# One group of leaky activations and its maximum moved behind ScalarE's two copies of the propagation's result

## The chip, the cores and the metric

The kernel runs on one core of a Trainium2 chip. Times are device microseconds (us) of a whole execution. TensorE, VectorE, ScalarE, GpSimd and SyncE are PE, DVE, ACT, POOL and SP in the profile; PEld is TensorE's weight load.

## The reference

Two graph layers work on 128 graphs of 128 nodes with 512 features, in float32. Layer 0 is graph attention with 8 heads, layer 1 a hypergraph convolution through a hidden width of 1024; each adds its input and normalizes.

```python
# layer 0: attention
dense = leaky_relu(e_self[..., :, None] + e_neigh[..., None, :], 0.2)
dense = dense + NEG_BIG * (1.0 - A)
att = softmax(dense, axis=-1)
out = relu(einsum('bhij,bhju->bhiu', att, feats) + b)
x = layernorm(x + out)
# layer 1: two hypergraph convolutions
h = layer_norm(relu(hypergraph_conv(x, adj, W1, b1)))
x = layernorm(x + hypergraph_conv(h, adj, W2, b2) + x)
```

## The kernel before

Graphs go in pairs, 64 of them, through a software pipeline that works on up to five pairs at once. The program is a list of steps with a lag (in pairs) and a time within a period; the list is sorted by (pair + lag) * 38.6 + time and issued. The times are no measurements: they only fix the order on each engine, and each engine keeps that order.

The steps of attention that matter: GpSimd adds the mask `neg` to the scores `nb`, ScalarE applies the leaky function, VectorE takes the maximum, ScalarE the exponential. Each is split into four groups (g = graph of the pair, q = half of the heads). The code here and below is shortened: lines that the argument does not need are left out, `...` stands for the rest of a line, and the comments are added.

```python
def masked(p, s, g, q):      # GpSimd, one instruction of 128x512
    nc.gpsimd.tensor_tensor(t, t, neg..., op=ALU.add)
def leaky(p, s, g, q):       # ScalarE, four instructions of 128x128
    for h in range(q * HH, (q + 1) * HH):
        nc.scalar.activation(t, t, AF.Prelu, bias=s["ft"][:, g, h, 0:1], alpha=SLOPE)   # (pair 0's special case cut)
def largest(p, s, g, q):     # VectorE, one reduction; exponential needs it
    nc.vector.tensor_reduce(s["nm"][:, g, hs], scores(p, s, g, hs)..., ALU.max, negate=True)

for (g, q), tm, (lag, tl), (lagx, tx), te, tt in (
    ((0, 0), 31.0, (1, 33.2), (1, 36.1), 2.7, 18.1), ((0, 1), 32.2, (1, 35.0), (1, 36.7), 4.6, 18.15),
    ((1, 0), 34.2, (1, 37.5), (2, 2.0), 7.8, 21.5), ((1, 1), 35.4, (2, 6.0), (2, 7.3), 7.9, 21.55),
):
    at(1, tm, masked, g, q); at(lag, tl, leaky, g, q); at(lagx, tx, largest, g, q)
    at(2, te, exponential, g, q)   # (rest of the loop cut)
```

The hidden product of an earlier pair stands at the same place of the period. TensorE makes the propagation `pz`, ScalarE copies it to `zT` (one copy for each graph), GpSimd forms four differences `zS`, and TensorE makes seven products in the order 1, 2, 6, 5, 7, 4, 3. Products 1 and 2 read graph 0 of zT alone; the third one issued, number 6, reads zS's second difference and adds to the bank `phX`, of which ScalarE must have copied product 1 first.

```python
at(3, 0.0, propagate, 0);  at(3, 0.9, propagate, 1)   # TensorE: pz
at(3, 1.1, z_evict, 0);    at(3, 2.0, z_evict, 1)     # ScalarE: zT <- pz
for i, t in enumerate((2.7, 3.4, 4.1, 4.8)):
    at(3, t, z_sums, i)                               # GpSimd: zS
chain("ph", 3, (2.0, 3.8, 5.6, 7.35, 9.1, 12.65, 14.4,   # TensorE: the seven products
                4.0, 7.5, 11.0), hidden, HALF)           # ScalarE: three copies of phX
rhs = {1: b[0][0], 2: b[0][1], 3: b[1][1], 4: t[:, 3], 5: t[:, 0], 6: t[:, 1], 7: t[:, 2]}[i]

@step(0, 38.4)
def mask(p, s):              # GpSimd; masked() reads it a period later
    nc.gpsimd.tensor_scalar(s["neg"], s["a"], -1.0, BIG, op0=ALU.add, op1=ALU.mult)
```

## Time and profile before

| | before |
|---|---|
| time, median of 3 runs | 2595.87 us |
| busy share PE / PEld / DVE / ACT / POOL | 97 / 88 / 74 / 59 / 71 % |
| steady period of a pair | 39.78 us |
| TensorE's idle time before the first hidden product | 56.3 us in 61 waits |

A group's line in the profile has the source line, engine, operation, tiles and count, then busy time and mean ns of one, then the idle time of the engine in front of the group and what ended it. Only idle time of the engine that bounds the kernel costs anything. The prediction below shows these lines; here is one view that it only mentions, the chain of work that ended last (shares of the span, by engine and by source line), of the kernel before:

```profile
PE 68%; ACT 13%; DMA 7%; issue 6%; DVE 2%; POOL 2%; SPq 1%; DVEq 0%; POOLq 0%; ACTq 0%
```

TensorE carries most of it, ScalarE the next largest part.

### The profile page before, as it was taken

The numbers are of one execution on the slowest core, as the hardware profiler recorded it, in microseconds if no ns is written. First come the engines' busy times: TensorE is split into PE (matmuls) and PEld (weight loads), VectorE is DVE, ScalarE is ACT, GpSimd is POOL, SyncE is SP. The second block draws the span as 40 slices with busy tenths as digits, with TensorE's granted clock in tenths as the row PEclk, the third lists the DMA queues.
The fourth block names the chain that finished last, engine by engine and source line by source line (L and its number), as shares of the span: only waits on it lengthen the run. The fifth ranks groups of instructions, "written<-read, shape, count | busy, mean of one in ns | idle before, by whom it ended". The sixth has DMA issues, their size and how long they took to land.

```text
span 2594.2 us, 48549 instructions
## 1 busy us (share of the span) xinstructions
PE 2513.1 (97%) x16349; PEld 2272.8 (88%) x16349; DVE 1915.8 (74%) x4332; ACT 1537.0 (59%) x4481; POOL 1833.0 (71%) x2058
## 2 busy tenths in 40 slices
PE   7999999999999999999999999999999999999998
PEld 5888888888888888888888888888888888888897
DVE  7877777777777777777777777777777777777765
ACT  4565665655655656656556566565565565665653
POOL 5777767776777677767766776777677767776774
PEclk9999999999999999999999999999999999999999
DMA  6544444445444454444444444444444444444431
GB/s 186 131 131 132 136 135 140 132 123 144 127 131 140 131 139 133 126 146 129 126 144 131 132 134 137 140 130 124 144 127 132 138 133 140 133 125 141 132 111 54
DMA packets 420840, 343.76 MB, mean 133 GB/s; under 512 B 141272, under 2 KB 370160, under 8 KB 420592
## 3 DMA queue, kind: packets, MB, share of 16 engines
q1 hardware_dynamic: 417120, 336.19, 43.8%
q10 hardware_dynamic: 3472, 4.47, 0.5%
q8 instruction: 131, 2.15, 0.3%
q14 instruction: 117, 0.96, 0.1%
HBM read 238.83 MB, written 101.71 MB: 131 GB/s over the span
## 4 chain that ended last, share of the span: by engine, by line
PE 68%; ACT 13%; DMA 7%; issue 6%; DVE 2%; POOL 2%; SPq 1%; DVEq 0%; POOLq 0%; ACTq 0%
PE phX L792 18%; PE phW L792 9%; PE pfX L473 8%; ACT nb L592 8%; PE pav L662 7%; PE pyX L473 6%; DMA x<-in_x_dram 6%; PE phY L792 4%; PE pq L919 4%; PE pfW L473 4%; PE pyY L473 3%; PE pfY L473 2%; ACT y L734 2%; POOL rsa L709 1%; ACT zT L769 1%
## 5 line engine op out<-in xcount | busy, mean ns | idle before, releaser
L792 PEld LDWEIGHTS phX<-zS,w_sb 128*128 128x128 f32 x3072 | 363.1, 192 | 33.0 <-issue 31.5
L329 ACT COPY py<-pyX 128x257 f32<-128x257 f32 x189 | 70.8, 375 | 539.2 <-PE pyX L473 513.6
L792 PE MATMUL phX<-zS,w_sb 128*128 128x128 f32 x3072 | 374.4, 275 | 2.2 <-POOL xS L455 1.3
L845 POOL TENSOR_TENSOR sq<-sq 128x512 f32<-128x512 f32 (+2 forms) x384 | 343.8, 895 | 37.6 <-ACT sq L833 17.5
L576 POOL TENSOR_TENSOR nb<-nb,neg 128x512 f32<-128x512 f32 x256 | 318.3, 1276 | 12.5 <-DMA nb<-rd 12.5
L592 ACT ACTIVATE nb<-nb,ft 128x128 f32<-128x128 f32 x1020 | 317.2, 388 | 7.1 <-POOL nb L576 7.1
L606 ACT ACTIVATE nb<-nb,nm 128x128 f32<-128x128 f32 x1024 | 320.5, 394 | 0.4 <-DVE nm L598 0.4
L709 POOL TENSOR_TENSOR rso<-veo,mhalf 128x2 f32<-128x2 f32 x63 | 44.2, 701 | 354.9 <-DVE veo L707 354.9
L598 DVE TENSOR_REDUCE nm<-nb 128x4 f32<-128x512 f32 x256 | 174.6, 683 | 116.0 <-ACT nb L592 56.4
L662 PEld LDWEIGHTS pav<-ft,eT 128*128 128x128 f32 x2048 | 248.3, 192 | 8.4 <-DVE eT L639 0.8
L662 PE MATMUL pav<-ft,eT 128*128 128x65 f32 x2048 | 242.5, 272 | 0.0
L473 PE MATMUL pyX<-w_sb,hS 128*128 128x257 f32 x1008 | 242.5, 382 | 0.0
L473 PE MATMUL pyX<-w_sb,h 128*128 128x257 f32 x1008 | 239.5, 380 | 0.5 <-ACT py L329 0.5
L822 ACT ACTIVATE h<-h,vecs 128x128 f32<-128x128 f32 x768 | 238.5, 392 | 2.2 <-DVE h L807 2.2
L473 PE MATMUL pyW<-w_sb,hS 128*128 128x256 f32 x1008 | 238.6, 378 | 0.2 <-DVE y L876 0.2
L473 PEld LDWEIGHTS pyW<-w_sb,hS 128*128 128x128 f32 x1008 | 190.7, 189 | 27.9 <-DVE y L876 0.7
L686 POOL TENSOR_TENSOR y<-y,b_bc 128x512 f32<-128x512 f32 x128 | 162.8, 1272 | 70.9 <-DVE y L677 70.9
L473 PEld LDWEIGHTS pyX<-w_sb,h 128*128 128x128 f32 x1008 | 186.4, 190 | 25.5 <-ACT py L329 0.9
L473 PEld LDWEIGHTS pyX<-w_sb,hS 128*128 128x128 f32 x1008 | 186.1, 190 | 24.3
L792 PE MATMUL phX<-zT,w_sb 128*128 128x128 f32 x1024 | 132.7, 283 | 56.3 <-ACT zT L769 56.3
L329 ACT COPY ph<-phX 128x512 f32<-128x512 f32 x192 | 112.5, 586 | 118.1 <-PE phX L792 118.1
L792 PEld LDWEIGHTS phX<-zT,w_sb 128*128 128x128 f32 x1024 | 120.7, 194 | 68.1 <-ACT zT L769 68.0
(167 smaller groups left out, 5778.4 us busy)
## 6 DMA issues: line engine op xcount, KB each, us to landing
nb<-rd SPq DMA_DIRECT2D x127, 512.0 KB, 6.7
ed<-nb SPq DMA_DIRECT2D x126, 512.0 KB, 2.6
eb<-ed SPq DMA_DIRECT2D x504, 128.0 KB, 2.9
x<-in_x_dram SPq DMA_DIRECT2D x64, 512.0 KB, 9.5
out_dram<-o SPq DMA_DIRECT2D x63, 512.0 KB, 2.8
xb<-in_x_dram SPq DMA_DIRECT2D x248, 128.0 KB, 3.1
a<-in_adj_dram SPq DMA_DIRECT2D x64, 128.0 KB, 8.2
w<-in_adj_dram SPq DMA_DIRECT2D x128, 64.0 KB, 7.3
```

The costliest lines, as they stand in the source:

```text
L329: nc.scalar.copy(t[:, :n], s[kind, "X"][:, :n])
L473: nc.tensor.matmul(to[:, :n], lhs[:, k, :], rhs[:, k, :n], start=bool(start) and k == 0, stop=(k == nk - 1), skip_group_check=True,)
L576: nc.gpsimd.tensor_tensor(t, t, neg[:, :, None, :].to_broadcast([P, NB, HH, B]), op=ALU.add)
L592: nc.scalar.activation(t, t, AF.Prelu, bias=s["ft"][:, g, h, 0:1], alpha=SLOPE)
L598: nc.vector.tensor_reduce(s["nm"][:, g, hs], scores(p, s, g, hs).rearrange("p b h j -> p h b j"), AX.XY, ALU.max, negate=True,)
L606: nc.scalar.activation(t, t, AF.Exp, bias=s["nm"][:, g, h:h + 1])
L662: nc.tensor.matmul(t[:, h * (U + 1):(h + 1) * (U + 1)], s["eT"][:, g, q * HH + h, :], s["ft"][:, g, q * HH + h, 2:], start=True, stop=True,)
L686: nc.gpsimd.tensor_tensor(s["y"][:, g, :], s["y"][:, g, :], b0_bc, op=ALU.add)
L792: nc.tensor.matmul(to[:, m * N:(m + 1) * N], w[:, k, m * P:(m + 1) * P], rhs[:, k, :], start=bool(start) and m == 0 and k == 0, stop=(k == ...
L822: nc.scalar.activation(dst[:, k, :], src[:, k, :], AF.Relu, bias=b1_sb[:, c:c + 1])
L845: nc.gpsimd.tensor_tensor(t[:, :n, :], t[:, :n, :], t[:, n:2 * n, :], op=ALU.add)
L919: nc.tensor.matmul(s["pq", g], s["R"][:, g, :], s["y2"][:, g, :, :QU], start=True, stop=True)
```

## The change

The intent is to let ScalarE copy zT before the leaky group of graph 1, heads 0 to 3, so that TensorE's first hidden product starts sooner. The group's maximum follows it in the program.

```diff
-        ((1, 0), 34.2, (1, 37.5), (2, 2.0), 7.8, 21.5), ((1, 1), 35.4, (2, 6.0), (2, 7.3), 7.9, 21.55),
+        ((1, 0), 34.2, (2, 2.05), (2, 2.1), 7.8, 21.5), ((1, 1), 35.4, (2, 6.0), (2, 7.3), 7.9, 21.55),
```

## The prediction

> **What bounds the kernel now.** I read the page's busy shares first, then the groups of TensorE by their idle time, then the chain of waits, then the timeline of one steady period of each engine.
>
> ```profile
> PE 2513.1 (97%) x16349; PEld 2272.8 (88%) x16349; DVE 1915.8 (74%) x4332; ACT 1537.0 (59%) x4481; POOL 1833.0 (71%) x2058
> ```
>
> TensorE (PE) is busy 97% of 2594.2 us, so about 81 us of the span is idle there. The kernel is 64 graph pairs in a software pipeline; from about 138 us to 2485 us each pair takes 39.78 us (the first matmul of phX starts at 1252.13 and 1291.91). The TensorE groups with idle time in front show where the idle part lies (idle is the second number after the bar):
>
> ```profile
> L792 PE MATMUL phX<-zT,w_sb 128*128 128x128 f32 x1024 | 132.7, 283 | 56.3 <-ACT zT L769 56.3
> L757 PE MATMUL pz<-R,y 128*128 128x128 f32 x1024 | 126.2, 277 | 6.0 <-ACT y L734 6.0
> ...
> L473 PE MATMUL pfX<-w_sb,xT 128*128 128x264 f32 x496 | 134.2, 393 | 0.0
> ```
>
> 56.3 us stand before the first hidden product of each pair, ended by ScalarE's copy of the propagation's result (zT, L769). Nearly every other group shows 0 to 2 us; the next largest, 8.1 us, is the first load. The chain of waits gives the same as a count: the wait occurs 61 times, and the weight loads see it as 68.0 us.
>
> ```profile
> PEld phX L792 <- ACT zT L769: 68.0, 61, 3.0
> ...
> PE phX L792 <- ACT zT L769: 56.3, 61, 2.8
> ```
>
> One of the 61 is 2.84 us (at 97.01 us, start-up); the other 60 are 0.88 to 0.90 us each. One period in the middle, from the timeline (start, length):
>
> ```profile
> 1289.08 1.95 PE L757 MATMUL pz<-R,y 128*128 128x128 f32 x16
> 1289.86 0.35 ACT L874 COPY y<-pyX 128x256 f32<-128x256 f32 x1
> 1290.11 1.28 ACT L592 ACTIVATE nb<-nb,ft 128x128 f32<-128x128 f32 x4
> 1291.29 1.05 ACT L769 COPY zT<-pz 128x512 f32<-128x512 f32 x2
> 1291.91 2.05 PE L792 MATMUL phX<-zT,w_sb 128*128 128x128 f32 x16 [0.88 <-ACT zT L769]
> 1292.23 1.28 ACT L606 ACTIVATE nb<-nb,nm 128x128 f32<-128x128 f32 x4
> 1292.90 1.15 POOL L780 TENSOR_TENSOR zS<-zT 128x256 f32<-128x256 f32 x1
> 1294.13 0.73 POOL L780 TENSOR_TENSOR zS<-zT,zS 128x256 f32<-128x256 f32 x1
> ...
> 1295.58 1.95 PE L792 MATMUL phX<-zS,w_sb 128*128 128x128 f32 x16
> ```
>
> The reader should see that four leaky activations (L592) stand between the copy of y and the two copies of zT, while TensorE's result for the first copy is ready early: the 16 matmuls of pz start 0.112 us apart, so graph 0's eight end at about 1289.08 + 7 x 0.112 + 0.275 = 1290.14. Those four activations are exactly the group that the change moves (graph 1, heads 0 to 3).
>
> **What the Trainium skill says.** "Perfetto Trace Analysis", section "Identifying the Most-Contended Engine", says that matmul busy time is a poor measure and that weight-load busy share is better; here that is 88%, so the choice of engine stands, with less certainty than 97% suggests. Its "Optimization Strategy" says to find the gaps on that engine and make what ends them start sooner, which is the change's intent. The same page, "DVE / Act Engine Instruction", puts semaphore propagation outside an instruction's recorded window; the trace agrees: phX starts a median of 0.052 us after the first zT copy ends, and I use 0.05 us for every hand-over. "SBUF — State Buffer", "Who interferes with whom", says that a VectorE instruction with two SBUF inputs and a GpSimd instruction that reads SBUF exclude one another. The trace agrees: the first zS subtraction takes 1.15 us here, where y's scaling runs on VectorE until 1293.46, and the second, undisturbed, 0.73.
>
> **The change part by part.** Nothing is added or removed: 62 x 4 activations and 62 reductions (pairs 2 to 63; the first two pairs have times or scaling of their own) get a new place. Their engine time is unchanged.
>
> On ScalarE the order becomes copy of y, two copies of zT, leaky group, exponentials. The y copy ends at 1290.21; graph 0's pz is ready at about 1290.14 + 0.05. So the first zT copy starts near 1290.2 instead of 1291.29 and, at 0.57 us, ends near 1290.77. TensorE would start phX back to back at the last pz matmul plus one step. In the 60 steady periods phX starts 1.167 us after the last pz matmul starts; one step is 0.112. **Ceiling: 1.167 - 0.112 = 1.055 us**, and the restart also costs something: the 32 matmuls from phX's first to the first on zS take 3.675 us where 32 steps are 3.576, so 0.10 us more is spared if no stall is left. The ceiling is 1.15 us a period, 69 us in all.
>
> It will not be reached, because of what comes next on TensorE. The third product needs zS's second difference, by GpSimd. That one ends at 1294.86, and not because zT was late: GpSimd works without a pause from 1284.99 (its power for rsa, four maskings, the small ops for rsh, the mask, then zS), with no wait for zT before zS: the second zT copy has ended at 1292.34, zS starts at 1292.90 as soon as the mask ends. What starts this block is VectorE's vea, which follows pyY's evaluation at 1281.76, itself released by TensorE. From pyY to pz TensorE has no pause, so GpSimd's zS keeps its distance to pz when zT comes early. Measured against phX's old start, zS's second difference ends at +2.968 us (median of the steady periods) and the third product starts at +3.675: today 0.707 us of slack.
>
> With phX at -1.055, the third product would be due at -1.055 + 3.576 = +2.521. zS lets it start at 2.968 + 0.05 = +3.02. **A new wait of about 0.50 us** replaces the 0.89 us one, with its own restart of 0.10 us. Net: 3.675 - (3.02 + 0.10) = **0.555 us a period**, x 60 = 33.3 us.
>
> Start-up period at 97.01 us: the gap of 2.84 us loses the four activations' 1.17 us (ScalarE's y copy ends there at 95.32, zT starts at 96.40); add 1.2 us. In the last changed period (2524.01) TensorE already starts phX without a gap: 0. Sum: 34.5 us. Predicted: 2595.9 - 34.5 = **2561 us**, a ratio of 0.987.
>
> What moves beside it: the second zT copy must wait for pz's end (1291.03), so ScalarE idles about 0.35 us and the leaky group ends near 1292.8. Its maximum on VectorE starts today at 1293.39, after y's scaling, so it still does not wait. The first phX copy comes at about 1293.95, ends at 1294.5, still ahead of the third product's overwrite at 1294.93. The next leaky group ends near 1296.85, and the second phX copy starts near 1297.05, which is TensorE's time; ScalarE's slack before it (0.64 us today) is used up, yet not overdrawn. VectorE before the second h sum loses its 0.21 us wait and comes about 0.36 us late relative to TensorE, but ScalarE works on the first relu group meanwhile, and VectorE waits 0.97 us for TensorE at the next h sum.
>
> **The rivals.** First, the full gain: zS does not bind, and 60 x 1.15 us make 2527 us (2.7% faster). For it: the change removes the only repeated TensorE gap. Against: the zS times above; it needs GpSimd to be early, and nothing in its 10 us block before zS is moved. It would also be right if the lengths shown for GpSimd are rough by half a microsecond.
>
> Second, the leaky group and its maximum become late work: ScalarE's extra idle and the chain leaky, exponential, phX copy delay the third product's bank or the store and re-read of the exponentials. ScalarE's slack in the stretch is 0.48 + 0.64 us today, of which about 0.35 is lost to waiting for pz and 0.5 because TensorE comes earlier. A shortfall of 0.3 us a period would leave about 2579 us. Against it: exponentials of graph 0 are ready earlier than before, by roughly the period's gain.
>
> Third, the pipeline is held by a transfer: nb's load must land before the masking. For: a large part of the chain that ended last is put down to an x load. Against: GpSimd waits for nb only once, at start-up (12.5 us), and in each period it waits 2.39 us for VectorE's vea. With a transfer bound the time would stay at 2596.
>
> **Range and chances.** The most likely size error is the hand-over and where zS ends, 0.1 to 0.2 us a period, 6 to 12 us in all. The second rival gives the upper side, half of the first the lower. So 2548 to 2577 us. Faster by over 2% needs less than 2544 us, 0.86 us a period: the zS bound would have to be mostly absent, 0.10. Slower by over 2% would need a new wait of over 1.7 us a period: 0.02. The rest is 0.88.
>
> **What would show it right or wrong.** The wait of phX on zT should fall from 56.3 us to nearly nothing (under 5), and a new wait of phX on POOL zS, about 60 times and 0.4 to 0.5 us each (25 to 30 us), should stand in its place. In the timeline zT's copies should start about 0.6 us before pz's last matmul with leaky after them, GpSimd should have no gap between its mask and zS, and the period should be near 39.22 us. I am wrong if no wait on zS appears (then the gain is nearer 60 us), if the first phX copy on ScalarE ends later than zS, or if VectorE's maximum waits for leaky and pushes the h sum behind phX.

## The result and the profile after

| | before | after |
|---|---|---|
| median, same rounds (4 runs each) | 2596.82 us | 2560.72 us |
| lowest to highest | 2595.8 to 2597.81 | 2559.9 to 2561.77 |
| ratio (95% interval) | | 0.9861 (0.9844 to 0.9878) |
| steady period, median | 39.778 us | 39.213 us |

Ratios are the mean time of one kernel's runs over that of the other's of the same rounds, so they are not quite the ratio of the medians quoted. The kernel is 1.4% faster, and clear of the noise.

Busy time on the page of the changed kernel:

```profile
PE 2516.7 (98%) x16349; PEld 2275.8 (89%) x16349; DVE 1914.3 (75%) x4332; ACT 1539.8 (60%) x4481; POOL 1832.7 (72%) x2058
```

The instructions are the same and each engine's busy time stays within 4 us; the shares rise because the span fell by 34.3 us. TensorE's groups (idle time is the second number after the bar):

```profile
L792 PE MATMUL phX<-zS,w_sb 128*128 128x128 f32 x3072 | 380.7, 277 | 19.0 <-POOL zS L780 17.2 <-POOL xS L455 1.3 <-ACT ph L329 0.5
...
L792 PE MATMUL phX<-zT,w_sb 128*128 128x128 f32 x1024 | 127.9, 278 | 1.7 <-ACT zT L769 1.7
```

The wait for zT fell from 56.3 to 1.7 us, and a wait for GpSimd's zS, which was not there before, stands in front of the products that read zS. The view of the waits counts it (us in total, times, longest):

```profile
PEld phX L792 <- POOL zS L780: 28.8, 61, 0.5
...
ACT zT L769 <- PE pz L757: 24.1, 66, 1.6
...
PE phX L792 <- POOL zS L780: 17.2, 61, 0.3
```

One steady period on the timeline of the changed kernel (start, length, engine):

```profile
1272.14 1.95 PE L757 MATMUL pz<-R,y 128*128 128x128 f32 x16
1272.93 0.35 ACT L874 COPY y<-pyX 128x256 f32<-128x256 f32 x1
...
1273.23 0.59 ACT L769 COPY zT<-pz 128x512 f32<-128x512 f32 x1
...
1273.92 2.00 PE L792 MATMUL phX<-zT,w_sb 128*128 128x128 f32 x16
...
1274.12 0.59 ACT L769 COPY zT<-pz 128x512 f32<-128x512 f32 x1 [0.31 <-PE pz L757]
...
1274.61 1.28 ACT L592 ACTIVATE nb<-nb,ft 128x128 f32<-128x128 f32 x4
...
1275.04 0.97 POOL L363 TENSOR_SCALAR neg<-a 128x256 f32<-128x256 f32 x1
...
1275.98 1.16 POOL L780 TENSOR_TENSOR zS<-zT 128x256 f32<-128x256 f32 x1
...
1277.22 0.72 POOL L780 TENSOR_TENSOR zS<-zT,zS 128x256 f32<-128x256 f32 x1
...
1277.99 2.05 PE L792 MATMUL phX<-zS,w_sb 128*128 128x128 f32 x16 [0.29 <-POOL zS L780]
```

phX follows pz at once. The mask and the two differences on GpSimd keep their place relative to pz: the second difference ends at 1277.22 + 0.72 = 1277.94, 0.05 us before the third product starts. Over the steady periods it ends 4.123 us after the last pz matmul starts, against 4.135 before; the third product starts a median of 0.053 us after it, against 0.706 before. The chain that ended last now has GpSimd where it had ScalarE:

```profile
PE 66%; POOL 23%; issue 8%; DVE 2%; DMA 1%; ACT 0%; SPq 0%; POOLq 0%; DVEq 0%; ACTq 0%
```

Where the 34.3 us between the two profiled spans came from, by the starts of phX on the timeline: the third pair's phX comes 1.6 us earlier (138.36 to 136.75), the 59 periods up to the 62nd pair's are 33.2 us shorter (2346.85 to 2313.64), and what follows it is 0.6 us longer (108.96 to 109.53), of which 0.4 us is the new wait in one more period (38.80 to 39.22 us).

### The profile page after: what moved, and what is told of

The parts are those of the page before. It is cut to its first block, busy times and chain, and to the rows that moved or that the text cites.

```text
span 2559.9 us, 48549 instructions
## 1 busy us (share of the span) xinstructions
PE 2516.7 (98%) x16349; PEld 2275.8 (89%) x16349; DVE 1914.3 (75%) x4332; ACT 1539.8 (60%) x4481; POOL 1832.7 (72%) x2058
## 4 chain that ended last, share of the span: by engine, by line
PE 66%; POOL 23%; issue 8%; DVE 2%; DMA 1%; ACT 0%; SPq 0%; POOLq 0%; DVEq 0%; ACTq 0%
PE phX L792 14%; POOL nb L576 11%; PE pyX L473 9%; PE phW L792 9%; PE pfX L473 9%; PE pav L662 8%; POOL zS L780 4%; PE pq L919 4%; PE pyY L473 4%; PE pfW L473 4%; POOL neg L363 2%; PE pfY L473 2%; POOL rsh L905 2%; POOL rsa L709 2%; DVE y L876 1%
## 5 line engine op out<-in xcount | busy, mean ns | idle before, releaser
L792 PE MATMUL phX<-zS,w_sb 128*128 128x128 f32 x3072 | 380.7, 277 | 19.0 <-POOL zS L780 17.2
L598 DVE TENSOR_REDUCE nm<-nb 128x4 f32<-128x512 f32 x256 | 174.6, 683 | 179.5 <-ACT nb L592 117.4
L627 DVE STREAM_TRANSPOSE eT<-eb 128x512 f32<-128x512 f32 x252 | 163.1, 684 | 0.8 <-DMA eb<-ed 0.7
L833 ACT ACTIVATE sq<-h 128x512 f32<-128x512 f32 x256 | 160.7, 629 | 2.1
L455 POOL TENSOR_TENSOR hS<-h 128x512 f32<-128x512 f32 x126 | 158.6, 1277 | 2.3 <-ACT h L822 2.3
```

The costliest lines, as they stand in the source:

```text
L627: nc.vector.transpose(s["eT"][:, g, hs, :].rearrange("p h (b i) -> p h b i", b=NB), s["eb", g][:, :, hs, :].rearrange("p b h j -> p h b j"),)
L792: nc.tensor.matmul(to[:, m * N:(m + 1) * N], w[:, k, m * P:(m + 1) * P], rhs[:, k, :], start=bool(start) and m == 0 and k == 0, stop=(k == ...
L833: nc.scalar.activation(s["sq"][:, g, q * KH // 2:(q + 1) * KH // 2, :], hid(s, g, q), AF.Square, scale=DH ** -0.5,)
```

## The experiments

The main theory: TensorE's wait for zT was on the path, the change removed it whole, and about half of the gain was given back because zS on GpSimd, which the change does not move, became the wait. The rivals: that ScalarE's order (its idle time before the second copy, the later copy of phX) is the limit and zS came last by chance; that more work on GpSimd costs time anywhere. Eight kernels were run, each in three rounds besides its profiled run; all gave correct results.

| run | median us | ratio to before (95%) | steady period us |
|---|---|---|---|
| mask_later | 2539.82 | 0.9779 (0.9765 to 0.9794) | 38.867 |
| between | 2561.6 | 0.9863 (0.9848 to 0.9878) | 39.226 |
| before_mask_later | 2596.44 | 0.9999 (0.9984 to 1.0014) | 39.777 |
| both | 2533.35 | 0.9754 (0.9737 to 0.977) | 38.759 |
| mask_twice | 2584.12 | 0.995 (0.9935 to 0.9964) | 39.580 |
| before_mask_twice | 2597.02 | 0.9999 (0.9984 to 1.0014) | 39.777 |
| behind_phx | 2560.83 | 0.9862 (0.9845 to 0.9878) | 39.214 |
| behind_phx_mask_later | 2527.9 | 0.9734 (0.9719 to 0.9749) | 38.667 |

The kernel before had medians of 2596.6 us in the rounds of the first four and 2597.37 us in those of the last four.

### mask_later: GpSimd's mask out of zS's way

On the changed kernel. The mask goes behind the four xS sums of its pair (6.1 to 8.2 in the program's times). The first two pairs, which have no xS sums, keep their place.

```diff
-    @step(0, 38.4)
     def mask(p, s):
...
+    at(0, 38.4, mask, until=2)
+    at(1, 8.3, mask, since=2)
```

> The changed kernel, with GpSimd's mask (0.97 us in front of zS) moved behind the four xS sums of its pair, where GpSimd has over 5 us free. Main theory, that zS's second difference is what the third product waits for: zS comes 0.5 us or more earlier, the wait of phX on zS falls from 17.2 us (matmuls) and 28.8 us (weight loads) to under 3 us each, and the period falls from 39.22 us to 38.7 to 38.85; the first copy of phX, which ends within 0.07 us of the third product, may show as a small wait. Time 2530 to 2540 us. Rival, that the order on ScalarE (its 0.31 us idle before the second zT copy, the later phX copy) is the limit and zS only came last by chance: the wait gets ScalarE's name, and the time stays at 2555 to 2562.

Measured 2539.82 us, at the upper edge of what was expected; the period of 38.867 us is just above it. The wait on zS is gone from the view of waits. Its timeline shows what remains:

```profile
1264.70 1.95 PE L794 MATMUL phY<-zT,w_sb 128*128 128x128 f32 x16
...
1265.90 0.57 ACT L329 COPY ph<-phX 128x512 f32<-128x512 f32 x1
...
1266.62 2.02 PE L794 MATMUL phX<-zS,w_sb 128*128 128x128 f32 x16
```

Sixteen matmuls take 16 x 0.112 = 1.79 us to issue, so the third product was due at 1266.49 and came at 1266.62. zS's second difference had ended a median of 0.88 us earlier; ScalarE's copy of phX ended at 1266.47. So zS was the limit, and the copy on ScalarE is the next one, 0.125 us later than the issue rate allows plus 0.07 us in the product's second matmul (0.184 us after the first instead of 0.112). The copy's hand-over is 0.144 us in the median, against 0.053 for zT and zS; which part makes it longer is open. That it is the copy is argued here; behind_phx_mask_later tests it.

### between: half of the reordering

On the changed kernel; the leaky group goes between the two copies of zT.

```diff
-        ((1, 0), 34.2, (2, 2.05), (2, 2.1), 7.8, 21.5), ...
+        ((1, 0), 34.2, (2, 1.5), (2, 2.1), 7.8, 21.5), ...
```

> The changed kernel, with the leaky group between the two zT copies instead of behind both: only one half of the change's reordering. Main theory: TensorE needs only the first copy for phX, and zS is held by GpSimd's own work and not by the second copy (which would end about 0.5 us before zS starts), so the time equals the changed kernel's, 2559 to 2563 us, and ScalarE's wait for pz before the second copy (24.1 us in all) is gone. Rival, that both copies had to come forward, or that ScalarE's idle costs time: slower by over 8 us in the first case, faster by over 5 us in the second.

Measured 2561.6 us, the changed kernel's time. ScalarE's wait for pz fell to 5.4 us, and TensorE's wait on zS stayed:

```profile
PE phX L792 <- POOL zS L780: 17.9, 61, 0.3
```

The first copy alone made the change's gain, and ScalarE's idle time before the second copy costs nothing as long as zS is late.

### before_mask_later: the second cure without the first

The same edit of the mask, on the kernel before.

> The kernel before, with only GpSimd's mask moved as in mask_later. Main theory: zS had 0.707 us of slack there and phX's start waited for zT, so earlier zS is worth nothing: 2594 to 2599 us. Rival, that GpSimd's load before zS costs time by itself (contention with VectorE's scaling of y, say) whatever the order on ScalarE: 10 us or more faster.

Measured 2596.44 us, no change. TensorE still waits 56.3 us for zT, and zS's slack before the third product grew to 1.180 us in the median. The mask's move is worth 21 us only after the leaky group has gone (2560.72 to 2539.82, medians of different rounds).

### both: group between the copies, mask later

> mask_later and between together on the changed kernel. Main theory: with zS early and the first phX copy about 0.35 us earlier too, TensorE runs from pz through all products without a gap: the period is 38.66 us (39.22 less 0.444 of wait and 0.10 of restart), 2525 to 2531 us, and faster than mask_later by up to 9 us. Rival (ScalarE's order is the limit): no better than between.

Measured 2533.35 us, 6.5 us better than mask_later but 2.4 us above the expected range; the period is 38.759 us, not 38.66. Its timeline:

```profile
1261.14 0.56 ACT L771 COPY zT<-pz 128x512 f32<-128x512 f32 x1
...
1261.78 0.81 POOL L782 TENSOR_TENSOR zS<-zT 128x256 f32<-128x256 f32 x1 [0.57 <-ACT zT L771]
...
1262.67 1.06 POOL L782 TENSOR_TENSOR zS<-zT,zS 128x256 f32<-128x256 f32 x1
...
1263.79 2.04 PE L794 MATMUL phX<-zS,w_sb 128*128 128x128 f32 x16
```

With the mask out of the way GpSimd is free before the second copy of zT, which the leaky group now delays: it waits 0.57 us for it. zS's second difference ends at 1263.73, only 0.06 us before the third product. No gap shows between the products, yet the product's second matmul comes 0.20 us after its first, instead of 0.112. That is the missing 0.09 us. The run taught that the order between, harmless while zS is held by the mask, is not harmless any more.

### mask_twice and before_mask_twice: more work in front of zS

The mask is computed twice with the same values, once on each kernel.

```diff
         nc.gpsimd.tensor_scalar(s["neg"], s["a"], -1.0, BIG, op0=ALU.add, op1=ALU.mult)
+        nc.gpsimd.tensor_scalar(s["neg"], s["a"], -1.0, BIG, op0=ALU.add, op1=ALU.mult)
```

> The changed kernel with GpSimd's mask done twice (the same values again), so that GpSimd carries more in front of zS. Main theory (zS sets the third product): each 0.1 us that zS comes later costs 0.1 us a period. The second mask takes 0.4 us alone; part of it may take the place of the time that zS's first difference now stands blocked (1.16 us against 0.73). So 0.25 to 0.8 us a period, 15 to 50 us slower than the changed kernel: 2576 to 2611 us; and the wait of phX on zS grows by the same amount as zS's delay in the trace. Rival (zS came last by chance): 2561 us, within 5 us.

Measured 2584.12 us, 23.4 us above the changed kernel (medians of different rounds). GpSimd's timeline in mask_twice:

```profile
1284.52 0.97 POOL L363 TENSOR_SCALAR neg<-a 128x256 f32<-128x256 f32 x1
1285.57 0.72 POOL L364 TENSOR_SCALAR neg<-a 128x256 f32<-128x256 f32 x1
1286.26 0.72 POOL L781 TENSOR_TENSOR zS<-zT 128x256 f32<-128x256 f32 x1
1287.06 0.73 POOL L781 TENSOR_TENSOR zS<-zT,zS 128x256 f32<-128x256 f32 x1
```

The second mask took 0.72 us, where 0.4 was expected, and spared the first difference its blocked time (0.72 instead of 1.16). Relative to pz, zS's second difference ends 4.491 us after pz's last matmul starts instead of 4.123: 0.368 us later. The period grew by 39.580 - 39.213 = 0.367 us. The delay arrives one for one, and the wait of phX on zS grew by as much, 0.37 us each (17.2 to 39.5 us in 61 waits):

```profile
PE phX L793 <- POOL zS L781: 39.5, 61, 0.7
```

> The kernel before with the mask done twice. Main theory: zS's second difference has 0.707 us of slack there, less 0.05 us of hand-over; a delay of 0.3 to 0.6 us is hidden: 2595 to 2600 us; only a delay over 0.65 us would show, by its excess. Rival, that more GpSimd work costs time anywhere: slower by the same 15 to 50 us as mask_twice is against the changed kernel.

Measured 2597.02 us against 2597.37 for the kernel before in the same rounds: nothing. zS ends at the same 4.491 us there, a delay of 0.356 us, and its slack falls from 0.706 to 0.350 us. The same work on the same engine costs 23 us in one kernel and shows no cost in the other.

### behind_phx and behind_phx_mask_later: the group behind the copy of phX as well

```diff
-        ((1, 0), 34.2, (2, 2.05), (2, 2.1), 7.8, 21.5), ...
+        ((1, 0), 34.2, (2, 4.05), (2, 5.95), 7.8, 21.5), ...
```

> The changed kernel with the leaky group moved on behind ScalarE's first copy of phX, and its maximum behind the first h sum; mask where it was. The first phX copy then comes over 0.5 us before it is needed. Main theory: zS still holds the third product, so no gain: 2558 to 2564 us, wait of phX on zS about 17 us. Rival (the leaky group on ScalarE is still in the way): faster by 10 us or more.

Measured 2560.83 us: no gain, wait of phX on zS 17.3 us. ScalarE's order is not the limit while zS is.

> behind_phx together with the mask moved behind the xS sums. mask_later lost 0.2 us a period to the first phX copy (third product 0.126 us late, 0.08 of restart), and the run with the group between the zT copies lost 0.10 because zS started later. Here neither should be left: period 38.66 to 38.69 us, 2525 to 2530 us, the fastest of all. If the maximum, now late, holds the exponentials or the h sum instead, 2535 us or more with a new wait named on ScalarE or VectorE.

Measured 2527.9 us (2527.67 to 2528.14), the fastest of all, 2.7% below the kernel before of the same rounds and, by the medians of different rounds, 1.3% below the changed one. The wait for zS has gone from its groups of TensorE (the 2.0 us left are three waits, which the kernel before has as well, at 2.2 us):

```profile
L794 PE MATMUL phX<-zS,w_sb 128*128 128x128 f32 x3072 | 374.4, 275 | 2.0 <-POOL neg L362 1.3 <-ACT ph L329 0.7
```

zS ends 0.748 us before the third product, the copy of phX about 1.0 us before it, and the steps from pz to phX, from product to product and within the third product are all 0.112 us. Together with mask_later this shows that the copy of phX was what mask_later still waited for: the mask stands alike in both, zS ends at the same place (2.98 us after pz's last matmul starts), and only the leaky group, and with it the copy, moved. The periods differ by 0.200 us, which is the 0.125 and 0.07 us seen in mask_later.

## Why the prediction was right

**The time.** 2561 us was predicted and 2560.72 measured; the range of 2548 to 2577 held.

**The gap that closes.** The step from pz to phX fell from 1.167 to 0.112 us as foreseen, and the first zT copy started at 1273.23, 0.69 us before phX and 0.58 before pz's last matmul (0.6 was written).

**The new wait.** zS's place relative to pz was assumed to stay; it moved by 0.012 us. mask_twice shows that a delay of zS reaches the period one for one, and mask_later, together with before_mask_later, shows that zS and not the load of GpSimd as such was the limit.

**The sum.** Predicted gain 0.555 us a period, measured 0.565. Its parts differ a little from those written. The new wait in front of the third product is a step of 0.556 instead of 0.112 us, so 0.444, not 0.50: the missing 0.05 is lost already in phX's second matmul (0.159 us after the first, instead of 0.112), though phX itself starts without a gap. So only 0.054 of the old restart's 0.10 us was spared: 1.055 + 0.054 - 0.444 - 0.101 = 0.564. The restart cost of 0.10 us was inferred from the length of 32 matmuls; it shows in the second matmul after a wait (0.213 us in both kernels). Start-up gave 1.6 us instead of 1.2, the end took 0.6 that was counted as 0. The mechanism held term by term, but that the total came within 1 us is in part luck: these errors cancel.

**Where the text was inexact.** It said that the new wait would show as 0.4 to 0.5 us each and 25 to 30 us in all. Weight loads show 28.8 us; the matmul row shows 17.2, 0.28 each. The matmul row counts idle time from the end that it records for the matmul before, 0.275 us after its start, while my 0.50 counts from the step; 0.556 - 0.275 = 0.281. The text should have said which row.

**What the hand-over is.** The prediction timed it to the first matmul and added a restart. The weight load in front of that matmul is what waits; it starts 0.05 us after the zT copy or the zS difference ends, and the second matmul follows that end by 0.266 us in the median wherever the product waited, and in no steady period of the ten kernels by less than 0.265. So in these kernels such a result costs time when it comes less than 0.266 - 0.112 = 0.154 us before its product is due, even if no gap shows: 0.107 us before phX cost the 0.047, and 0.067 us before the third product cost both its 0.09. Read so, zS's slack before was 0.706 - 0.154 = 0.552 us, and with the 0.012 us that zS moved it gives 0.564, against 0.565 measured.

**The rivals.** The full gain did not come in the changed kernel; its estimate of 2527 us was met by a kernel in which zS and the copy of phX are early as well (2527.9), though not by its sum: there 59 periods gained 65.5 us and the start 2.5, where 60 x 1.15 = 69 was written. The rival of ScalarE's slack fell with between and behind_phx, which give its idle time back or move the group and gain nothing. That VectorE's maximum would not be late held for this group. The next leaky group did use up the slack: the maximum after it stands idle longer, and VectorE's waits for leaky rose from 56.4 to 117.4 us in all, without reaching TensorE. The transfer rival fell with the result: the time did not stay at 2596 us.

## What to carry to other kernels

When one wait in front of the busiest engine is removed, the gain is the distance to the next thing that the engine needs, read as slack on the timeline before: here 1.15 us of gap and 0.55 us of slack in zS, its hand-over taken off. A delay of that next thing costs nothing before the change while it fits the slack, and its full length after it, so cures that measure as worthless alone (the mask's move) should be tried again once the first wait is gone. Read gaps by the step from one matmul's start to the next, not by busy share alone.

## What the Trainium skill lacked or had wrong

- "Perfetto Trace Analysis", "DVE / Act Engine Instruction": it puts semaphore propagation outside the recorded window but gives no length there. The runs show 0.053 to 0.054 us in the median from the end of the ScalarE copy of zT or a GpSimd difference to the start of the matmul that waited, and 0.144 us from the copy of phX to the matmul that adds to that bank (mask_later); the reason for the longer one is open.
- "TensorE: Matmul & The Clock Gate", "Back-to-back issue gap" and the phases before it: what resuming after a wait costs the matmul behind the first one is not given there. After a wait for zT or zS the second matmul stands 0.213 us behind the first instead of 0.112, 0.266 to 0.268 us behind the release. After a wait for the copy of phX (mask_later) it is 0.184 us, 0.328 behind the release.
- "Perfetto Trace Analysis", "Identifying the Most-Contended Engine": nothing wrong; the warning on matmul busy time held. In mask_later TensorE is recorded busy for 38.87 us of a 38.87 us period, yet behind_phx_mask_later has a period of 38.667.
- "SBUF — State Buffer", "Who interferes with whom": nothing wrong. With the mask gone from its front, zS's first difference starts before y's scaling on VectorE (1.01 against 1.08 us after phX in one period of mask_later) and is no longer held (0.73 us instead of 1.16). Now the scaling is (a mean of 1218 ns, against 838 before), and so is zS's second difference behind it (1.06 us instead of 0.73).
